# Square roots and residual sums as three-operand instructions on VectorE, and a new order for the scan layer's groups

## The chip, the cores and the metric

One core of a Trainium2 chip runs the whole kernel. The metric is the device time of one launch in microseconds, and less is better. The kernel before was timed ten times: the median is 15846.93 us, the runs lie between 15842.52 and 15853.14 us.

The core has five engines with queues of their own, each working strictly in its order: TensorE for matmuls (PE in the profile, its weight loads PEld), VectorE (DVE), ScalarE (ACT), GpSimd (POOL) and SyncE (SP, which here only issues DMAs). An instruction that waits holds up everything behind it on its engine.

## The reference

The input x is float32 of shape (8, 64, 128, 128). Four layers follow, each of the form x = x + layer(group norm of x):

```python
x = x + _L0_conv_ref(_gn(x), ...)   # offsets from 1x15 and 15x1 convolutions, deformable 3x3, batch norm, relu
x = x + _L1_conv_ref(_gn(x), L1_conv_weight)   # 3x3 convolution
x = x + _L2_conv_ref(_gn(x), ...)   # state-space scan over rows and over columns, both ways, then a 128 -> 64 fusion
x = x + _L3_conv_ref(_gn(x), ...)   # down by 4, nearest neighbours in a window, 3x3, attention, up by 4
```

The change is about the third layer. For each of two directions d it does

```python
fx = _layer_norm(x, ln1_g[i], ln1_b[i])        # over the 64 channels of a pixel
h = _s5_scan(fx, ...)                          # x[l] = lam_bar * x[l-1] + B u[l], forwards and backwards
x = jax.nn.gelu(h) + fx                        # the residual sum
fx2 = _layer_norm(x, ln2_g[i], ln2_b[i])       # the root: 1 / sqrt(var + 1e-5)
return fx2 @ ff_enc[i].T @ ff_dec[i].T + fx2
```

## The kernel before

Two images make a pair (2 x 64 channels on 128 partitions), so there are four pairs. Layer 0 runs first for all pairs: 9216 indirect gathers by POOL, each weighted and summed by VectorE. Then, pair by pair: `conv3x3` (layer 1; beside it, as `aside`, layer 3 of the pair before), `first_norm` with the first direction's backward scan (`back`) beside it, and `Turns`, which holds the rest of layer 2.

`Turns` works on two "ways" (the two directions), each cut into 16 groups of eight image rows or columns. One group is some fifty steps. They are put into one list with a due time each, the list is sorted by due time, and the instructions are emitted in that order (`run`, under `manual_schedule`, so nothing reorders them). A due time is the group's number times a length plus an entry of a table: `BESIDE` and the first number of `LENGTH` for the first way's 16 groups, beside which the second way's backward scan runs (`behind`, steps with a b at the end of the name); `ALONE` and the second number for the second way's 16 groups, beside which, in all pairs but the last, the next pair's input is loaded, passed through relu and added (`load`, `relu`, `join`, `sums`). The tables only set the order; a factor on a whole table with its length changes nothing.

A group's steps that matter below, by their names in the tables:

- `pv` (PE) applies the input matrix; `pt` (ACT) is `pv` with its halves swapped; `u` and `v` (VectorE, L1301, outputs `uu`, `uv`) multiply them by cosine and sine tables; `uv` (POOL, L1501) adds them; `scan` (VectorE, L1322) runs two first-order recurrences. `ub`, `vb`, `uvb` (L1555) and `scanb` are the same for the backward scan.
- `xm`, `xmb` (POOL, L1362) and `xt`, `xtb` (VectorE, L1367) rotate the states of the two scans back, `xs`, `xsb` (POOL, L1513 and L1512) subtract; `pya`, `pyb`, `pyc` (PE) apply the output matrices, for two halves h = 0 and 1.
- `gelu0`, `gelu1` (ACT), and `sum0`, `sum1` (L1522), the residual sums: both on VectorE in `ALONE`; in `BESIDE` `sum0` on VectorE and `sum1` on POOL.
- `pc` (PE) mixes, `sq` (ACT) squares and copies, `var` (VectorE, L1411) sums the squares. `root` (VectorE) is one call of `rsqrt` for both halves, 16 numbers on each partition: in the kernel before twelve instructions (L112, L114, L116 and three rounds of L120, L121, L122), each using the result of the one before it. `ms0` and `ms1` (POOL, L1416) scale by it, `tp` (PE) transposes, `add0` and `add1` (VectorE, L1428) add to the image.
- `stats` (L1436) and `sums` (L597) are bn_stats of finished rows on VectorE; `join` (POOL, L593) adds 128x1024 elements.

`rsqrt` is also called 32 times in `first_norm` with 32 numbers on a partition, read from PSUM (`by_pixel`), and about twenty times elsewhere with one number.

Of the kernel before, what the change touches and what calls it, by code (L numbers as in the profile page):

```python
# [9 lines left out]
F32 = mybir.dt.float32  # L10
I32 = mybir.dt.int32
AF = mybir.ActivationFunctionType
ALU = mybir.AluOpType
# [3 lines left out]
P = 128  # L17
# [25 lines left out]
class Net:  # L43
# [32 lines left out]

    def setup_constants(self):
        nc, const = self.nc, self.const
        with self.tc.tile_pool(name="setup", bufs=1) as sp:
            pid = self.iota(sp, "pid", [(0, 1)], mult=1)  # L80
            col = self.iota(sp, "col", [(1, P)])
            self.ident = const.tile([P, P], F32, name="ident")
            nc.vector.tensor_scalar(self.ident, col, pid, None, ALU.is_equal)

            pair_p = self.part_bits(sp, "pair_p", ALU.logical_shift_right, 1)
            pair_c = self.iota(sp, "pair_c", [(1, C), (0, 2)])
            self.pairmean = const.tile([P, P], F32, name="pairmean")
            nc.vector.tensor_scalar(self.pairmean, pair_c.rearrange("p a b -> p (a b)"), pair_p, 0.5, ALU.is_equal, ALU.mult)

            half_p = self.part_bits(sp, "half_p", ALU.bitwise_and, C - 1)  # L90
            half_c = self.iota(sp, "half_c", [(0, 2), (1, C)])
            self.halfmean = const.tile([P, P], F32, name="halfmean")
            nc.vector.tensor_scalar(self.halfmean, half_c.rearrange("p a b -> p (a b)"), half_p, 0.5, ALU.is_equal, ALU.mult)

            img_p = self.part_bits(sp, "img_p", ALU.logical_shift_right, 6)
            img_c = self.iota(sp, "img_c", [(1, 2), (0, C)])
            mean = sp.tile([P, P], F32, name="mean")
            nc.vector.tensor_scalar(mean, img_c.rearrange("p a b -> p (a b)"), img_p, 1.0 / C, ALU.is_equal, ALU.mult)
            self.center = const.tile([P, P], F32, name="center")
            nc.vector.tensor_sub(self.center, self.ident, mean)  # L100
            self.imgmean = const.tile([P, 2, 16], F32, name="imgmean")
            nc.vector.tensor_copy(self.imgmean, mean.rearrange("p (a b) -> p a b", b=C)[:, :, 0:16])
# [3 lines left out]
    def rsqrt(self, pool, v, n, eps, tag):  # L106

        nc = self.nc
        ve = pool.tile([P, n], F32, tag=tag + "_ve", name=tag + "_ve")

        to = ve if len(v.shape) == 2 else ve.rearrange("p (a b c) -> p a b c", b=v.shape[2], c=v.shape[3])
        nc.vector.tensor_scalar_add(to, v, eps)  # L112
        sh = pool.tile([P, n], I32, tag=tag + "_sh", name=tag + "_sh")
        nc.vector.tensor_single_scalar(sh, ve.bitcast(I32), 1, op=ALU.logical_shift_right)  # L114
        yi = pool.tile([P, n], I32, tag=tag + "_y", name=tag + "_y")
        nc.vector.tensor_scalar(yi, sh, -1.0, float(0x5F3759DF), ALU.mult, ALU.add)  # L116
        y = yi.bitcast(F32)
        t = pool.tile([P, n], F32, tag=tag + "_t", name=tag + "_t")
        for _ in range(3):
            nc.vector.tensor_mul(t, y, y)  # L120
            nc.vector.scalar_tensor_tensor(t, t, -0.5, ve, ALU.mult, ALU.mult)  # L121
            nc.vector.scalar_tensor_tensor(y, t, 1.5, y, ALU.add, ALU.mult)  # L122
        return y

# [1109 lines left out]
class Scan:  # L1234
# [146 lines left out]
    def hidden(self, g, h, py):  # L1381
        hs = self.wp.tile([P, 2, NB], F32, tag=f"h{h}", name=self.name(f"h{h}", 0, g), bufs=1)
        self.nc.scalar.activation(hs, py, AF.Gelu_apprx_tanh)
        return hs

    def mixed(self, g, h, hs, tag):

        nc = self.nc
        pc = [self.net.ps.tile([P, 4, 2, C], F32, tag=tag, name=self.name(f"pc{e}", h, g)) for e in range(2)]
        for m in range(2):  # L1390
            for i in range(2):
                for e in range(2):
                    rows = slice(e * C, (e + 1) * C)
                    both = self.mix[rows].rearrange("p (k e c) -> p k e c", k=2, e=2)[:, :, e]
                    nc.tensor.matmul(pc[e][:, 2 * m + i], lhsT=hs[rows, i, m * P : (m + 1) * P], rhs=both, start=True, stop=True)  # L1395
        return pc
# [52 lines left out]
class Turns:  # L1449


    BESIDE = dict(
        fx0=-42.405, fx1=-41.515, send=-40.807, zb=-28.652, pv=-26.364, pt=-21.441, u=-23.400, v=-17.007, uv=-14.705, pn=-20.678, z0=-18.245,
        scan=-13.543, zbt=-19.316, zt=-11.695, xmb=-10.926, xm=-11.234, xtb=-12.091, xt=-6.973, xsb=-6.185, xs=-3.151, pya=1.153, pyb=1.983,
        pyc=4.135, gelu0=4.021, sum0=5.398, pc0=8.273, sq0=10.755, var0=11.167, ms0=31.030, tp0=31.405, add0=40.135, gelu1=8.596, sum1=10.354,
        pc1=11.923, sq1=13.839, var1=20.715, ms1=39.583, tp1=44.833, add1=47.931, root=27.330, fxb0=-33.141, fxb1=-33.784, sendb=-31.014, pvb=-23.283,
        ptb=-19.852, ub=-14.630, vb=-14.109, uvb=-13.836, pnb=-9.910, z0b=-8.486, scanb=-5.226, save=-1.631,
    )
    ALONE = dict(
        fx0=-40.919, fx1=-37.171, send=-26.823, zb=-13.844, pv=-23.784, pt=-19.725, u=-18.742, v=-17.490, uv=-15.840, pn=-19.028, z0=-15.748,  # L1460
        scan=-12.765, zbt=-11.653, zt=-8.893, xmb=-7.844, xm=-11.490, xtb=-10.053, xt=-8.474, xsb=-7.169, xs=-4.677, pya=-2.975, pyb=0.799,
        pyc=11.316, gelu0=0.529, sum0=4.375, pc0=12.259, sq0=16.063, var0=19.019, ms0=34.253, tp0=41.960, add0=45.498, gelu1=16.070, sum1=21.691,
        pc1=22.877, sq1=27.017, var1=30.598, ms1=34.057, tp1=40.614, add1=44.609, root=31.015, store=94.689, stats=96.794, load=29.367, relu=46.454,
        join=51.618, sums=92.183,
    )
    LENGTH = 18.003, 17.817

    def __init__(self, net, ways, follow):
        self.net, self.ways, self.follow, self.plan = net, ways, follow, []
# [2 lines left out]
    def at(self, G, what, fn, late=0.0):  # L1472

        long, short = self.LENGTH
        t = (self.BESIDE, self.ALONE)[G >= NG][what]
        self.plan.append((min(G, NG) * long + max(0, G - NG) * short + t + late, len(self.plan), fn))

    def group(self, w, g):

        s, nc, G = self.ways[w], self.net.nc, NG * w + g  # L1480
        c, last, alone = {}, self.made.get((w, g - 1)), G >= NG
        self.made[w, g] = c

        def put(what, fn, key=None):
            def do():
                r = fn()
                if key:
                    c[key] = r

            self.at(G, what, do)  # L1490
# [24 lines left out]
        xs = lambda: [(1, c["x1"][0]), (0, c["x0"][0])]  # L1515
# [1 line left out]
        put("pyb", lambda: s.products(g, 1, None, None, xs(), True), "py1")  # L1517
        put("pyc", lambda: s.products(g, 1, c["py1"], c["in"], [], False))
        for h in range(2):
            adds = nc.gpsimd if h and not alone else nc.vector  # L1520
            put(f"gelu{h}", lambda h=h: s.hidden(g, h, c[f"py{h}"]), f"hs{h}")
            put(f"sum{h}", lambda h=h, adds=adds: adds.tensor_add(c[f"hs{h}"], c[f"hs{h}"], c["in"][:, :, h, :]))  # L1522
            put(f"pc{h}", lambda h=h: s.mixed(g, h, c[f"hs{h}"], "y" if h and not alone else "x"), f"pc{h}")
            put(f"sq{h}", lambda h=h: s.emptied(g, h, c[f"pc{h}"]), f"sq{h}")
            put(f"var{h}", lambda h=h: s.variance(g, h, c[f"sq{h}"][0], c.get("var")), "var")
            put(f"ms{h}", lambda h=h: s.scaled(h, c[f"sq{h}"][1], c["y"]))
            put(f"tp{h}", lambda h=h: s.flipped(g, h, c[f"sq{h}"][1], ("small", "bs")[h]), f"tp{h}")
            put(f"add{h}", lambda h=h: s.added(g, h, c[f"tp{h}"]))
# [100 lines left out]
```

## Time and profile before

| what | us |
|---|---|
| median of ten runs | 15846.93 |
| the profiled execution | 15841.47 |
| its span | 15839.7 |
| layer 0's gathers, first to last issue | 139.5 to 11665.8 |
| `Turns`, second pair: first gelu to last bn_stats | 13112.1 to 13640.8 |
| one group there in `BESIDE`, gelu0 to gelu0, settled | 16.8 |
| one group there in `ALONE`, settled | 15.5 |

```text
PE 10342.7 (65%) x32760; PEld 3743.6 (24%) x32760; DVE 11800.7 (75%) x27321; ACT 3260.7 (21%) x5530; POOL 10285.4 (65%) x10572
```

The line gives, for each engine, the time it was busy, its share of the span and its instructions. Shares over the whole span mix stages that have different limits; in `Turns` the profile has to be read for itself. A timeline row gives the start, the duration, the engine, the source line, the operation, output and inputs, their shapes, a count, and in brackets how long the engine had been idle and what ended that. VectorE instructions that don't depend on each other overlap slightly: the next one's start comes some 0.08 us before the recorded end of the one before, so a step is counted from start to start.

### The profile page before, as it was taken

The numbers are of one execution on the slowest core, as the hardware profiler recorded it, in microseconds if no ns is written. First come the engines' busy times: TensorE is split into PE (matmuls) and PEld (weight loads), VectorE is DVE, ScalarE is ACT, GpSimd is POOL, SyncE is SP. The second block draws the span as 40 slices with busy tenths as digits, with TensorE's granted clock in tenths as the row PEclk, the third lists the DMA queues.
The fourth block names the chain that finished last, engine by engine and source line by source line (L and its number), as shares of the span: only waits on it lengthen the run. The fifth ranks groups of instructions, "written<-read, shape, count | busy, mean of one in ns | idle before, by whom it ended". The sixth has DMA issues, their size and how long they took to land. (4 is left out here: it accounts for less than half of the span.)

```text
span 15839.7 us, 121589 instructions
## 1 busy us (share of the span) xinstructions
PE 10342.7 (65%) x32760; PEld 3743.6 (24%) x32760; DVE 11800.7 (75%) x27321; ACT 3260.7 (21%) x5530; POOL 10285.4 (65%) x10572
## 2 busy tenths in 40 slices
PE   7864577447755553776656556664258788888886
PEld 2211122112211111221111111111123434434343
DVE  6777777777777777777777777777756858679587
ACT  1100111011100000110000000000016537366373
POOL 5777777777777777777777777777744506236052
PEclk9986798669877775987878778886569999999998
DMA  5444444345443333544333333333333433434434
GB/s 173 125 121 134 132 148 154 114 126 157 152 118 114 115 116 116 153 137 119 113 115 119 115 115 116 115 115 108 108 119 84 132 106 101 123 113 124 113 90 114
DMA packets 901297, 1933.56 MB, mean 122 GB/s; under 512 B 200060, under 2 KB 436996, under 8 KB 877572
## 3 DMA queue, kind: packets, MB, share of 16 engines
q0 software_dynamic: 442368, 1208.55, 26.3%
q1 hardware_dynamic: 383200, 679.50, 14.2%
q10 hardware_dynamic: 75044, 37.72, 1.3%
q8 instruction: 265, 4.34, 0.1%
q14 instruction: 420, 3.44, 0.1%
HBM read 1540.74 MB, written 208.10 MB: 110 GB/s over the span
## 5 line engine op out<-in xcount | busy, mean ns | idle before, releaser
L380 POOL DMA_INDIRECT g<-table,idx x9216 | 8718.3, 946 | 2822.9 <-issue 2631.7
L391 DVE TENSOR_TENSOR g<-g,corner_weights 128x256 f32<-128x256 f32 x9216 | 3765.4, 415 | 2713.4 <-DMA g<-table,idx 2674.2
L392 DVE TENSOR_REDUCE sm<-g 128x64 f32<-128x256 f32 x9216 | 5012.6, 579 | 9.0
L292 PE MATMUL po<-xe,wt 128*54 128x512 f32 (+3 forms) x8384 | 4307.1, 629 | 14.3 <-ACT ob L302 13.7
L398 PE MATMUL sp<-ident,sm 128*128 128x128 f32 x4096 | 1537.5, 380 | 4147.8 <-DVE sm L392 4133.5
L403 ACT COPY s<-sp 128x512 f32<-128x512 f32 x1024 | 598.6, 585 | 8703.1 <-PE sp L398 8702.8
L398 PEld LDWEIGHTS sp<-ident,sm 128*128 128x128 f32 x4096 | 630.6, 156 | 6710.2 <-DVE sm L392 5004.5
L292 PEld LDWEIGHTS po<-xe,wt 128*54 128x54 f32 x8384 | 904.3, 132 | 1354.1 <-issue 1070.8
L409 PE MATMUL yp<-s,wd 128*64 128x512 f32 (+1 forms) x2560 | 902.8, 714 | 25.6 <-ACT s L403 24.8
L924 POOL COPY l_yb<-ln_y 128x512 f32<-128x512 f32 x128 | 76.4, 637 | 1241.7 <-DVE ln_y L122 1241.7
L641 PE MATMUL c<-room,l_w 128*64 128x508 f32 (+1 forms) x3072 | 738.7, 606 | 44.1 <-DMA room<-nx 28.3
L1272 ACT ACTIVATE fx<-room,ln_b,ln_g 128x512 f32<-128x512 f32 x512 | 646.0, 1300 | 94.0 <-DMA in<-fx 76.2
L1288 PE MATMUL pv<-in,tabs 128*128 128x512 f32 x1024 | 546.4, 660 | 88.4 <-DMA in<-fx 43.1
L1378 PE MATMUL py<-in,outs 128*128 128x512 f32 x1024 | 519.5, 632 | 1.8 <-ACT ms L1405 1.7
L1378 PE MATMUL py<-x,outs 128*128 128x512 f32 x1024 | 477.7, 601 | 0.0
L1416 POOL TENSOR_TENSOR ms<-ms,ln_y 128x512 f32<-128x512 f32 x256 | 268.3, 1058 | 271.1 <-DVE ln_y L122 268.8
L1322 DVE TENSOR_TENSOR_SCAN z<-tabs,z,uu 128x256 f32<-128x256 f32 x512 | 405.9, 830 | 42.8 <-POOL uu L1338 40.2
L1395 PE MATMUL pc<-mix,h 64*128 64x128 f32 x4096 | 318.3, 297 | 135.7 <-DVE h L1522 95.8
L641 PEld LDWEIGHTS c<-room,l_w 128*64 128x64 f32 x3072 | 287.5, 139 | 384.8 <-issue 313.8
L402 PE MATMUL s<-ident,sm 128*64 128x128 f32 x512 | 176.6, 345 | 306.3 <-DVE sm L392 293.1
L643 DVE TENSOR_TENSOR room<-room,c 128x512 f32<-128x512 f32 x128 | 87.3, 684 | 372.0 <-PE c L641 368.8
L409 PEld LDWEIGHTS yp<-s,wd 128*64 128x64 f32 (+1 forms) x2560 | 261.6, 159 | 433.0 <-issue 316.3
(422 smaller groups left out, 10328.0 us busy)
## 6 DMA issues: line engine op xcount, KB each, us to landing
g<-table,idx POOLq DMA_INDIRECT x9216, 2.7
in<-fx SPq DMA_DIRECT2D x1024, 128.0 KB
xe<-in_x_dram SPq DMA_DIRECT2D x56, 1408.0 KB
table<-q SPq DMA_DIRECT2D x256, 256.0 KB
y<-ys SPq DMA_DIRECT2D x128, 256.0 KB
room<-in_x_dram SPq DMA_DIRECT2D x64, 512.0 KB
room<-nx SPq DMA_DIRECT2D x256, 128.0 KB
back<-z SPq DMA_DIRECT2D x128, 256.0 KB
```

The costliest lines, as they stand in the source:

```text
L292: nc.tensor.matmul(po[:, r0:r1, c0:c1], lhsT=wt[:, t, :], rhs=xe[:, row + r0 : row + r1, c0 + dx : c1 + dx], start=n == 0, stop=n == len(u ...
L380: nc.gpsimd.indirect_dma_start(out=tq[:, k, :], out_offset=None, in_=flat[i], in_offset=bass.IndirectOffsetOnAxis(ap=idx[:, at : at + 1], ...
L391: nc.vector.tensor_mul(t[:, ks], t[:, ks], w)
L392: nc.vector.tensor_reduce(sm[:, ks], t[:, ks].rearrange("p k q c -> p k c q"), axis=mybir.AxisListType.X, op=ALU.add)
L398: nc.tensor.transpose(sp[:, j, :], sm[:, j * P : (j + 1) * P], self.ident)
L403: nc.scalar.copy(st[i][:, :, m * P : (m + 1) * P], sp)
L409: nc.tensor.matmul(yp[half[i], :], lhsT=wd[rows, j, :], rhs=src[rows, :], start=j == 0, stop=j == 4)
L641: nc.tensor.matmul(o, lhsT=lt, rhs=mv, start=k < 2, stop=k >= len(calls) - 2)
L1272: self.nc.scalar.activation(fx[:, e].rearrange("p h (o m) -> p h o m", m=self.INNER), src, AF.Identity, bias=self.w["ln1_b"], scale=self.w ...
L1288: self.nc.tensor.matmul(pv, lhsT=self.tabs[:, at : at + P], rhs=fx[:, :, h, :], start=h == 0, stop=h == 1)
L1322: self.nc.vector.tensor_tensor_scan(z[:, i, 1 : NB + 1], decay, u[:, i, :], z[:, i, 0:1], ALU.mult, ALU.add)
L1378: self.nc.tensor.matmul(py, lhsT=lt, rhs=mv, start=first and n == 0, stop=n == len(calls) - 1 and (fx is not None))
```

## The change

`rsqrt` gets by without VectorE's one-input and two-operand forms: each of its instructions is now a scalar_tensor_tensor, (in0 op scalar) op in1. The logical shift disappears, since -0.5 times the bits, read as an integer, plus a constant does both steps. So eleven instructions stand where twelve stood. The constant comes from a one-column tile `magic`. Where the input has four dimensions (`first_norm`, in PSUM) the first instruction stays as it was. The residual sums on VectorE take the same form. Both tables and the lengths are replaced.

```diff
+        self.magic = const.tile([P, 1], F32, name="magic")
+        nc.vector.memset(self.magic, float(0x5F3759DF))
...
-        to = ve if len(v.shape) == 2 else ve.rearrange("p (a b c) -> p a b c", b=v.shape[2], c=v.shape[3])
-        nc.vector.tensor_scalar_add(to, v, eps)
-        sh = pool.tile([P, n], I32, tag=tag + "_sh", name=tag + "_sh")
-        nc.vector.tensor_single_scalar(sh, ve.bitcast(I32), 1, op=ALU.logical_shift_right)
+        if len(v.shape) == 2:
+            nc.vector.scalar_tensor_tensor(ve, v, eps, v, ALU.add, ALU.max)
+        else:
+            nc.vector.tensor_scalar_add(ve.rearrange("p (a b c) -> p a b c", b=v.shape[2], c=v.shape[3]), v, eps)
         yi = pool.tile([P, n], I32, tag=tag + "_y", name=tag + "_y")
-        nc.vector.tensor_scalar(yi, sh, -1.0, float(0x5F3759DF), ALU.mult, ALU.add)
+        nc.vector.scalar_tensor_tensor(yi, ve.bitcast(I32), -0.5, self.magic.to_broadcast([P, n]), ALU.mult, ALU.add)
...
         for _ in range(3):
-            nc.vector.tensor_mul(t, y, y)
-            nc.vector.scalar_tensor_tensor(t, t, -0.5, ve, ALU.mult, ALU.mult)
+            nc.vector.scalar_tensor_tensor(t, y, -0.5, y, ALU.mult, ALU.mult)
+            nc.vector.scalar_tensor_tensor(t, t, 1.0, ve, ALU.mult, ALU.mult)
             nc.vector.scalar_tensor_tensor(y, t, 1.5, y, ALU.add, ALU.mult)
...
+    def summed(self, hs, x, aside):
+        if aside:
+            self.nc.gpsimd.tensor_add(hs, hs, x)
+        else:
+            self.nc.vector.scalar_tensor_tensor(hs, hs, 1.0, x, ALU.mult, ALU.add)
...
     BESIDE = dict(
-        fx0=-42.405, fx1=-41.515, send=-40.807, zb=-28.652, pv=-26.364, pt=-21.441, u=-23.400, v=-17.007, uv=-14.705, pn=-20.678, z0=-18.245,
+        fx0=-45.652, fx1=-47.679, send=-42.514, zb=-23.890, pv=-31.014, pt=-22.829, u=-25.279, v=-19.908, uv=-18.338, pn=-21.924, z0=-20.467,
...
-    LENGTH = 18.003, 17.817
+    LENGTH = 21.546, 24.354
...
-            put(f"sum{h}", lambda h=h, adds=adds: adds.tensor_add(c[f"hs{h}"], c[f"hs{h}"], c["in"][:, :, h, :]))
+            put(f"sum{h}", lambda h=h: s.summed(c[f"hs{h}"], c["in"][:, :, h, :], h and not alone))
```

What the tables become on the two engines that matter, one settled period (steps of several groups):

```text
BESIDE  VectorE before  root xt var0 add1 u scanb v var1 ub vb add0 scan sum0 xtb
        VectorE after   root xt u var0 add1 scanb v ub vb var1 scan add0 sum0 xtb
        POOL before     ms0 xs uv ms1 uvb xm xmb sum1 xsb
        POOL after      ms0 xs ms1 uv uvb xm xmb sum1 xsb
ALONE   VectorE before  root u v var0 sums sum1 sum0 scan stats xtb add1 xt add0 var1
        VectorE after   root u v sum1 add0 stats scan var0 sums xtb xt sum0 add1 var1
        POOL before     ms1 ms0 uv xm xmb xsb xs join
        POOL after      uv ms1 xm xmb xsb ms0 xs join
```

On PE and ACT the order in `BESIDE` changes in a few places (pv before tp1; z0 and z0b later or earlier by some steps); in `ALONE` PE runs tp0 pn pya pyb pc1 tp1 pyc pv pc0, where it ran pyb tp1 pc1 tp0 pyc pv pc0 pya pn.

More of the change, by code (lines that the diff above doesn't have):

```diff
@@ L1452 @@
     BESIDE = dict(
-        fx0=-42.405, fx1=-41.515, send=-40.807, zb=-28.652, pv=-26.364, pt=-21.441, u=-23.400, v=-17.007, uv=-14.705, pn=-20.678, z0=-18.245,
-        scan=-13.543, zbt=-19.316, zt=-11.695, xmb=-10.926, xm=-11.234, xtb=-12.091, xt=-6.973, xsb=-6.185, xs=-3.151, pya=1.153, pyb=1.983,
-        pyc=4.135, gelu0=4.021, sum0=5.398, pc0=8.273, sq0=10.755, var0=11.167, ms0=31.030, tp0=31.405, add0=40.135, gelu1=8.596, sum1=10.354,
-        pc1=11.923, sq1=13.839, var1=20.715, ms1=39.583, tp1=44.833, add1=47.931, root=27.330, fxb0=-33.141, fxb1=-33.784, sendb=-31.014, pvb=-23.283,
@@ L1457 @@
-        ptb=-19.852, ub=-14.630, vb=-14.109, uvb=-13.836, pnb=-9.910, z0b=-8.486, scanb=-5.226, save=-1.631,
+        fx0=-45.652, fx1=-47.679, send=-42.514, zb=-23.890, pv=-31.014, pt=-22.829, u=-25.279, v=-19.908, uv=-18.338, pn=-21.924, z0=-20.467,
+        scan=-17.477, zbt=-21.716, zt=-10.595, xmb=-13.956, xm=-16.483, xtb=-12.386, xt=-6.541, xsb=-8.637, xs=-4.189, pya=3.246, pyb=4.850,
+        pyc=5.035, gelu0=4.068, sum0=8.411, pc0=10.360, sq0=12.619, var0=18.195, ms0=35.736, tp0=42.572, add0=49.502, gelu1=6.165, sum1=11.369,
@@ L1458 @@
+        pc1=13.025, sq1=19.116, var1=24.577, ms1=45.304, tp1=55.515, add1=62.138, root=32.998, fxb0=-39.102, fxb1=-39.291, sendb=-33.449, pvb=-27.769,
+        ptb=-22.659, ub=-19.512, vb=-19.321, uvb=-17.665, pnb=-14.526, z0b=-8.897, scanb=-1.320, save=0.599,
     )
     ALONE = dict(
-        fx0=-40.919, fx1=-37.171, send=-26.823, zb=-13.844, pv=-23.784, pt=-19.725, u=-18.742, v=-17.490, uv=-15.840, pn=-19.028, z0=-15.748,
-        scan=-12.765, zbt=-11.653, zt=-8.893, xmb=-7.844, xm=-11.490, xtb=-10.053, xt=-8.474, xsb=-7.169, xs=-4.677, pya=-2.975, pyb=0.799,
@@ L1462 @@
-        pyc=11.316, gelu0=0.529, sum0=4.375, pc0=12.259, sq0=16.063, var0=19.019, ms0=34.253, tp0=41.960, add0=45.498, gelu1=16.070, sum1=21.691,
-        pc1=22.877, sq1=27.017, var1=30.598, ms1=34.057, tp1=40.614, add1=44.609, root=31.015, store=94.689, stats=96.794, load=29.367, relu=46.454,
-        join=51.618, sums=92.183,
+        fx0=-51.767, fx1=-41.682, send=-37.725, zb=-16.016, pv=-29.340, pt=-19.974, u=-20.804, v=-19.806, uv=-19.540, pn=-22.227, z0=-19.605,
+        scan=-17.335, zbt=-15.589, zt=-14.503, xmb=-14.133, xm=-14.265, xtb=-11.591, xt=-10.011, xsb=-7.864, xs=-5.653, pya=4.831, pyb=7.800,
@@ L1465 @@
+        pyc=13.782, gelu0=9.353, sum0=14.661, pc0=20.405, sq0=30.528, var0=33.864, ms0=65.653, tp0=73.515, add0=78.834, gelu1=24.228, sum1=30.085,
+        pc1=33.967, sq1=41.979, var1=46.643, ms1=56.716, tp1=61.026, add1=65.309, root=48.888, store=88.626, stats=79.551, load=24.511, relu=38.822,
+        join=43.314, sums=107.607,
     )
-    LENGTH = 18.003, 17.817
+    LENGTH = 21.546, 24.354
     def __init__(self, net, ways, follow):
@@ L1519, in group @@
         for h in range(2):
-            adds = nc.gpsimd if h and not alone else nc.vector
             put(f"gelu{h}", lambda h=h: s.hidden(g, h, c[f"py{h}"]), f"hs{h}")
-            put(f"sum{h}", lambda h=h, adds=adds: adds.tensor_add(c[f"hs{h}"], c[f"hs{h}"], c["in"][:, :, h, :]))
+            put(f"sum{h}", lambda h=h: s.summed(c[f"hs{h}"], c["in"][:, :, h, :], h and not alone))
             put(f"pc{h}", lambda h=h: s.mixed(g, h, c[f"hs{h}"], "y" if h and not alone else "x"), f"pc{h}")
```

## The prediction

> **What bounds the kernel now.** The busy shares by stage come first. Here are two settled stretches of the second pair, six groups in BESIDE and ten in ALONE; columns: stretch, its length, busy time of PE, PEld, DVE, ACT and POOL with their instructions, granted clock, DMA share, GB/s.
>
> ```profile
> 13193.90:13294.60 100.70, 91.10 (x409) 47.20 (x408) 98.44 (x163) 77.95 (x145) 65.98 (x54) 0.97 0.38 95
> 13433.40:13588.70 155.30, 132.30 (x621) 70.95 (x620) 151.18 (x277) 101.35 (x200) 106.98 (x82) 0.95 0.50 153
> ```
>
> VectorE is busy 98% and 97%, and no VectorE row there has idle time of note before it: VectorE sets the pace. Next is PE; its work, from the starts of its rows with its waits taken out, is 14.7 us of BESIDE's 16.8 us and 12.5 us of ALONE's 15.5 us. The second view is the timeline of both engines around a root in BESIDE (start, duration).
>
> ```profile
> 13211.32 0.66 DVE L1522 TENSOR_TENSOR h<-h,in 128x512 f32<-128x512 f32 x1
> 13211.90 0.68 DVE L1367 TENSOR_TENSOR xt<-pt,tabs 128x512 f32<-128x512 f32 x1
> 13212.50 0.63 DVE L112 TENSOR_SCALAR ln_ve<-var 128x16 f32<-128x16 f32 x1
> 13213.17 1.20 DVE L114 TENSOR_SCALAR ln_sh<-ln_ve 128x16 int32<-128x16 int32 x1
> 13214.40 1.19 DVE L116 TENSOR_SCALAR ln_y<-ln_sh 128x16 int32<-128x16 int32 x1
> 13215.62 1.19 DVE L120 TENSOR_TENSOR ln_t<-ln_y 128x16 f32<-128x16 f32 x1
> 13216.85 0.18 DVE L121 SCALAR_TENSOR_TENSOR ln_t<-ln_t,ln_ve 128x16 f32<-128x16 f32 x1
> ...
> 13211.56 1.54 POOL L1362 TENSOR_TENSOR x<-z,tabs 128x512 f32<-128x512 f32 x1 [1.36 <-PE pn L1307]
> 13213.07 1.27 POOL L1362 TENSOR_TENSOR x<-zb,tabs 128x512 f32<-128x512 f32 x1
> 13214.30 1.26 POOL L1522 TENSOR_TENSOR h<-h,in 128x512 f32<-128x512 f32 x1
> 13215.52 1.27 POOL L1512 TENSOR_TENSOR x<-x,xt 128x512 f32<-128x512 f32 x1
> 13218.57 1.05 POOL L1416 TENSOR_TENSOR ms<-ms,ln_y 128x512 f32<-128x512 f32 x1 [1.79 <-DVE ln_y L122]
> ```
>
> Sixteen numbers take 0.17 us, but four of the root's instructions take 0.63 to 1.20, and each ends 0.02 or 0.03 us after a POOL instruction ends. POOL has four instructions queued ahead of ms0; when they are through, POOL waits for the root, and the other eight run freely. In ALONE the same is seen with POOL's `join`:
>
> ```profile
> 13506.86 0.28 DVE L112 TENSOR_SCALAR ln_ve<-var 128x16 f32<-128x16 f32 x1
> 13507.18 2.28 DVE L114 TENSOR_SCALAR ln_sh<-ln_ve 128x16 int32<-128x16 int32 x1
> 13509.49 0.17 DVE L116 TENSOR_SCALAR ln_y<-ln_sh 128x16 int32<-128x16 int32 x1
> ...
> 13505.84 1.27 POOL L1513 TENSOR_TENSOR x<-x,xt 128x512 f32<-128x512 f32 x1
> 13507.08 2.35 POOL L593 TENSOR_TENSOR room<-room,yr 128x1024 f32<-128x1024 f32 x1
> ```
>
> In these stretches L121 and L122, already three-operand, take 0.17 or 0.18 us every time. That looks like immunity, but they run when POOL has nothing left to do. Where one does start inside a POOL instruction, it waits too; in the first norm:
>
> ```profile
> 11991.03 1.30 POOL L1338 TENSOR_TENSOR uu<-uu,uv 128x512 f32<-128x512 f32 x1 [4.24 <-DVE ln_y L116]
> ...
> 11991.23 1.14 DVE L121 SCALAR_TENSOR_TENSOR ln_t<-ln_t,ln_ve 128x32 f32<-128x32 f32 x1
> ```
>
> It ends 0.04 us after POOL. This meeting occurs eight times in the scan layers (twice in each pair) and costs 1.14 to 1.15 us each time.
>
> **The change part by part.** *One instruction fewer in a root*: start to start, a free one is 0.21 us (13216.85 to 13217.06), on VectorE, which bounds: -0.21 us in each of 128 groups. In the first norm it is on the chain root, POOL copy, PE: 32 x 0.21 = -6.7 us if nothing covers it, 0 if the scan beside it does; I take the first. About twenty other roots are single: 20 x 0.2 = 4 us at most, and those in layer 0 lie beside gathers; I take 0.
>
> *The form*: with POOL idle a three-operand instruction takes what the others take (0.17 us). With POOL busy, eight meetings of eight show the wait, for 128x32 with two different inputs. That one tile given twice, or 128x512, waits too is shown for two-operand forms only: L120 (one tile twice) and L1522. So I take the wait as unchanged. Bounds: all gone, or all there.
>
> The Trainium skill bears on this, "SBUF — State Buffer", section "Who interferes with whom": an instruction of VectorE with two inputs in SBUF contends with a GpSimd instruction that reads SBUF, and this speaks against any gain from the form, for the cases that no row shows too. The section says as well that the loser "fully blocks" until the first finishes; a 128x512 instruction would then need its whole 0.7 us afterwards, while the rows show 0.54. By the rule the sum below, which has two long meetings more in each BESIDE group than the kernel before, would be 2 x 0.16 x 64 = 20 us longer; the rows decide.
>
> *The new order*, walked through with three prices from rows. A short instruction that meets POOL ends 0.04 us after it. A long one (scan, sum) ends 0.54 us after it: the scan at 13209.46 ends at 10.75, uvb at 10.21. POOL waits for a long one that is running (xm 1.54 instead of 1.27). Inputs from PSUM don't meet POOL: L1301 takes 0.68 us either way.
>
> BESIDE. Starts to starts, the old period is 12.75 of work and 4.05 of waits (root 3.5, scan 0.56) = 16.8. In the new order, let add0 start at 0, the scans having ended at 0.08. POOL's xm runs 0.24 to 1.51; sum0 comes at 1.13 and, waiting for xm, ends at 2.05; xmb, held by it, ends at 3.20. xtb runs 1.97 to 2.57. The root starts at 2.57 and meets xmb (to 3.24), sum1 (4.47) and xsb (5.70), three instead of four, then has eight free steps: xt starts at 7.3. ms0 ends at 8.6, xs at 9.8, and ms1, now next, at 10.84. xt, u, var0, add1 take until 10.23, so scanb meets ms1: 11.38 instead of 10.96. v, ub, vb, var1 end at 14.4; uv and uvb run 12.8 to 15.3, so scan meets uvb: 15.84. The next add0 starts at 16.4. **-0.4 us a group, x 64 = -26 us.** PE must be ready for pc0 at 2.2 + 16.4: from add1's end (10.3) pn and the three py take 7.5, so 17.8: 0.8 us to spare.
>
> ALONE with the next pair's input. Old: 12.95 of work + 2.55 of waits (L114 2.1, L112 0.1, sum1 0.35) = 15.5. New, from scan's end: var0, both sums and xtb until 2.4, xt until 3.0; xm, xmb, xsb run 0.16 to 3.9, so sum0 ends at 4.44; ms0, held by it, ends at 5.4, xs at 6.6, join at 8.95. add1 and var1 end at 6.07. The root meets xs (6.63) and join (8.96), nine free steps take it to 10.8; u, v until 12.0, sum1 12.6, add0 13.6, stats 14.8, scan 16.2. **+0.7 us a group, x 48 = +34 us.** Behind this wait on VectorE stand u and v, so pt, zbt and gelu0 on ACT, and tp1 on PE (after ms1): PE is then idle 3.7 us of 16.2, so it doesn't bind. The last pair has no join and no sums: the same walk gives 13.9 against 13.3 to 13.7 in the rows; +0.4 x 16 = +6 us.
>
> *Head, turn and tail of Turns*: fx, send, fxb, sendb come in the same order and start the same chain. At the turn the load of `outs` waits on SP for pyc of group 15, and the load of zb and a send stand behind it; VectorE is then idle 6.5 us (before 13368.42). In the new tables zb 16 is again due just after that load, so this stays: 0, +-3 us a pair. Fewer stats and sums are left for the tail; they filled waits for PE (0.5 and 1.2 us at 13611 and 13623): 0 to +3 us a pair.
>
> Sum: -6.7 - 26 + 34 + 6 = +7 us. Against its own execution: 15841.5 + 7 = 15849; that execution lies 5.5 us below the median, so **15855 us**. With +-0.4 us a group in BESIDE (26 us) and +-0.5 in ALONE (32 us), its own range is 15815 to 15895.
>
> **The rivals.** *Three operands are immune.* For it: L122 never waits in 480 executions. Against: the eight meetings. Then BESIDE would be bound by PE at 14.7 to 15 (-1.9 x 64 = -122) and ALONE by VectorE at 12.95 - 0.2 or PE, about 13 (-2.5 x 48, and -0.5 x 16): -128. With the first norm's -7 that is -257: 15590 us.
>
> *Slower: the fourth meeting stays.* The gain in BESIDE rests on xm running beside add0. If xm starts more than 1.1 us late (the row puts its release at pn on PE), xmb, sum1 and xsb all move back and the root meets four instructions, while ms1 and uvb still meet the scans: 16.4 + 1.05 = 17.45, +0.65 x 64 = +42, with ALONE's +40 and the first norm's -7: 15920 us. For it: PE's 0.8 us to spare is thin. Against: xm needs only scan and a free tile.
>
> *Faster: join comes late.* If relu on ACT is done only after the root has begun, join isn't there to meet it, and runs beside u and v, which read PSUM. The root then saves 2.1 us and sum1 loses some 0.5 to it: -1.6 x 48 = -77, so +7 - 77 = -70: 15777 us. For it: in ALONE of the second pair join waited for relu 10 us in all. Against: in the walk relu is done at 2.5 and join can't start before 6.6; it takes 4 us of delay before this decides.
>
> *The change doesn't do what it says*: the tables move only the order, and where all engines wait for VectorE the order gives the same sum. Then only the instructions count: -27 - 7, 15813 us.
>
> **How the numbers follow.** Forecast 0.54, immune 0.06, fourth meeting 0.23, late join 0.10, instructions only 0.07. Less than 0.2% (32 us) can't be told from no change here. The forecast splits into 0.05 faster, 0.35 within, 0.14 slower; immunity and the late join are faster, the fourth meeting is slower, and the last case lies at the edge, 0.04 and 0.03. Faster 0.25, same 0.38, slower 0.37. The range for 8 in 10 runs from 15775 (late join) to 15930 (fourth meeting); it leaves out immunity and what lies beyond those two.
>
> **What would show it.** In the new profile: L121-like rows of the root at 0.6 to 2.3 us, three a root in BESIDE and two in ALONE, each ending with POOL; sum0 at 0.9 us or more; gelu0 to gelu0 16.4 in BESIDE and 16.2 in ALONE; VectorE still 97% busy. Wrong: roots of eleven rows of 0.17 us beside busy POOL (immune), or idle time on VectorE in settled groups, ended by PE or ACT (an order that starves it).

## The result and the profile after

The kernel after takes 15933.85 us (median of 8 runs, 15928.52 to 15936.54) against 15847.59 us for the kernel before (28 runs): a ratio of 1.0054, 95% interval 1.0045 to 1.0063, so it is 86 us slower. Its profiled execution spans 15925.0 us, the one before 15839.7 us.

From the starts of the gelu rows, group 0 of a pair to group 0 of the next, the 85 us are made up like this (four pairs, 15 intervals each in BESIDE and in ALONE; "the end" is here and below the end of VectorE's last instruction, 5 us before the end of the span):

| stretch, summed over the pairs | before | after | difference |
|---|---|---|---|
| BESIDE, first to last gelu0 | 985.6 | 975.2 | -10 |
| turn, last gelu0 of BESIDE to first of ALONE | 83.7 | 88.0 | +4 |
| ALONE, first to last gelu0 | 869.9 | 996.4 | **+126** |
| from there to the next pair's first gelu0 (tail, group norm, convolution, first norm) | 1549.4 | 1524.6 | -25 |
| last gelu0 to the end | 240.8 | 229.9 | -11 |

All of the loss lies in ALONE. Settled, a group takes 16.6 us in BESIDE (16.8 before, 16.4 predicted); in ALONE it takes 17.8 us with the next pair's input (15.1 before, 16.2 predicted) and 15.4 us in the last pair (13.0 before, 13.9 predicted).

The busy times of two settled stretches of the second pair after, six groups in BESIDE and ten in ALONE, in the columns that the prediction used (length, then PE, PEld, DVE, ACT, POOL):

```profile
13201.70:13301.20 99.50, 88.93 (x409) 46.15 (x408) 95.48 (x157) 77.80 (x145) 67.52 (x54) 1.00 0.38 96
13451.60:13629.30 177.70, 142.32 (x623) 75.11 (x620) 160.09 (x269) 103.09 (x201) 114.70 (x83) 0.90 0.43 134
```

VectorE was busy 97% of ALONE; now it is 90%. It is no longer only slow, it stands idle. The timeline of one ALONE group after shows where, and which parts of the walk came true (VectorE, then ACT, then POOL):

```profile
13562.53 1.69 DVE L1391 SCALAR_TENSOR_TENSOR h<-h,in 128x512 f32<-128x512 f32 x1
...
13565.86 0.52 DVE L113 SCALAR_TENSOR_TENSOR ln_ve<-var 128x16 f32<-128x16 f32 x1
13566.42 2.27 DVE L117 SCALAR_TENSOR_TENSOR ln_y<-ln_ve,magic 128x16 int32<-128x16 int32 x1
13568.72 0.17 DVE L121 SCALAR_TENSOR_TENSOR ln_t<-ln_y 128x16 f32<-128x16 f32 x1
...
13570.48 0.68 DVE L1302 TENSOR_TENSOR uu<-pv,tabs 128x512 f32<-128x512 f32 x1
13572.51 0.69 DVE L1302 TENSOR_TENSOR uv<-pt,tabs 128x512 f32<-128x512 f32 x1 [1.34 <-ACT z L1317]
...
13564.23 0.59 ACT L1384 ACTIVATE h<-py 128x512 f32<-128x512 f32 x1
13571.26 1.15 ACT L1261 COPY pt<-pv 64x512 f32<-64x512 f32 x2 [6.44 <-DVE uu L1302]
...
13562.40 1.27 POOL L1519 TENSOR_TENSOR x<-x,xt 128x512 f32<-128x512 f32 x1
...
13565.08 1.27 POOL L1520 TENSOR_TENSOR x<-x,xt 128x512 f32<-128x512 f32 x1
13566.31 2.35 POOL L594 TENSOR_TENSOR room<-room,yr 128x1024 f32<-128x1024 f32 x1
```

The three-operand sum0 beside `xsb` takes 1.69 us, L113 beside `xs` 0.52, L117 beside join 2.27, and the root's other nine rows 0.17 or 0.18: these are the walk's meetings, one for one. What the walk doesn't have is the 1.34 us ahead of v (`uv`). It is put down to a tiny `z` copy, but that row ran at 13572.33, behind `pt`; what v reads is `pt`. And `pt`, two copies on ACT that swap the halves of `pv`, starts 0.09 us after u (`uu`) has ended, after ACT has stood idle for 6.44 us, though `pv` was ready on PE at 13564.05. In all 56 ALONE groups whose u lies between the first and the last gelu0 of ALONE, over the four pairs, `pt` starts 0.09 us after u's end; in the kernel before it started 1.9 to 6.5 us ahead of u's end. One such place of the kernel before (VectorE, then ACT), with v right behind u:

```profile
13526.99 0.68 DVE L1301 TENSOR_TENSOR uu<-pv,tabs 128x512 f32<-128x512 f32 x1
13527.59 0.68 DVE L1301 TENSOR_TENSOR uv<-pt,tabs 128x512 f32<-128x512 f32 x1
...
13522.07 1.15 ACT L1260 COPY pt<-pv 64x512 f32<-64x512 f32 x2
```

The rows of these copies over ten ALONE groups add it up, first before, then after:

```profile
L1260 ACT COPY pt<-pv 64x512 f32<-64x512 f32 x20 | 11.2, 558 | 6.4 <-PE pv L1288 5.9
L1261 ACT COPY pt<-pv 64x512 f32<-64x512 f32 x20 | 11.2, 558 | 64.4 <-DVE uu L1302 64.1
```

After, ACT is idle for 64 us ahead of these copies, all put down to u. The waits recorded in the trace say the same: after, the first `pt` copy of a group waits for VectorE and ACT, and u for PE alone; before, the copy waits for PE and for an older VectorE instruction, since it runs ahead of u, and it is u that waits for ACT. Both only read `pv`. So the schedule puts these two readers of one PSUM tile in the order in which they are issued, though they run on different engines; e3 and e9 below turn that order round. In the diff, ALONE's u went from 0.98 behind `pt` (-18.742 against -19.725) to 0.83 ahead of it (-20.804 against -19.974).

### The profile page after: what moved, and what is told of

Same layout as the page of the kernel before. It is cut to its first block, busy times and chain, and to the rows that moved or that the text cites. A ratio compares the mean times of both kernels' runs of the same rounds, so it can differ in the third digit from the quotient of the medians.

```text
span 15925.0 us, 121497 instructions
## 1 busy us (share of the span) xinstructions
PE 10367.6 (65%) x32760; PEld 3735.5 (23%) x32760; DVE 11779.7 (74%) x27142; ACT 3255.3 (20%) x5530; POOL 10329.2 (65%) x10572
## 5 line engine op out<-in xcount | busy, mean ns | idle before, releaser
L1508 POOL TENSOR_TENSOR uu<-uu,uv 128x512 f32<-128x512 f32 x128 | 184.7, 1443 | 448.3 <-DVE uv L1302 432.7
L1261 ACT COPY pt<-pv 64x512 f32<-64x512 f32 x512 | 285.7, 558 | 455.5 <-DVE uu L1302 353.1
```

## The experiments

Twelve kernels were run, in three sets: e1 to e4, e5 to e8, e9 to e12. In the second and third set, on another chip than the first, the gathers of layer 0, which no kernel here changes, took about 3000 us longer for every kernel, the kernel before among them (18892 and 18996 us); the later stages did not (BESIDE 16.6 us in e6 as in e3). So besides the ratio to the kernel before in the same set, the table gives the interval from the first gelu0 to the end of the one profiled execution of each kernel, and gelu0 to gelu0 (the median of a pair, its first interval left out; pairs one to three for ALONE, then the last pair).

| kernel | ratio, 95% interval | first gelu0 to end | BESIDE | ALONE | last ALONE |
|---|---|---|---|---|---|
| before | 1 | 3729.6 | 16.8 | 15.0-15.1 | 13.0 |
| after | 1.0054, 1.0045-1.0063 | 3814.1 | 16.6 | 17.8 | 15.4 |
| e1 operations alone | 0.9977, 0.9968-0.9986 | 3694.7 | 16.6 | 14.9-15.4 | 12.6 |
| e2 order alone | 1.0078, 1.0064-1.0092 | 3850.0 | 16.8 | 18.0 | 15.6 |
| e3 `pt` ahead of u | 1.0008, 0.9999-1.0017 | 3742.1 | 16.6 | 16.4 | 13.9 |
| e4 old ALONE | 0.9979, 0.9970-0.9988 | 3687.3 | 16.6 | 14.9-15.1 | 13.1 |
| e5 ms0 early | 0.9998, 0.9931-1.0064 | 3710.3 | 16.2 | 16.4 | 13.9 |
| e6 join late | 0.9956, 0.9908-1.0003 | 3734.9 | 16.6 | 15.7-16.1 | 13.9 |
| e7 both, old order | 1.0007, 0.9949-1.0065 | 3742.2 | 16.5-17.5 | 15.2-15.4 | 12.5 |
| e8 root clear | 1.0082, 1.0022-1.0142 | 3845.0 | 18.9 | 15.2-15.4 | 12.6 |
| e9 u ahead, old order | 1.0031, 1.0017-1.0045 | 3766.1 | 16.6 | 16.6 | 14.5 |
| e10 join on VectorE | 0.9961, 0.9944-0.9978 | 3647.9 | 16.6 | 13.8-14.1 | 12.5 |
| e11 and two more | 0.9979, 0.9963-0.9995 | 3661.4 | 16.6 | 13.9-14.1 | 12.9 |
| e12 and three more | 0.9961, 0.9948-0.9974 | 3647.5 | 16.5 | 14.0-14.1 | 12.8 |

**The two halves of the change, one at a time.** e1 has the new operations with both old tables and LENGTH; e2 has the old operations with the new ones.

> The tables of due times and LENGTH are those of the kernel before; only the operations are the changed kernel's (root in eleven three-operand instructions, sums on VectorE in three-operand form). Theory (the form waits for POOL as the two-operand form does, and only the instruction saved counts): 0.21 us less in each of 128 groups and up to 7 us less in the first norms: BESIDE 16.6 and ALONE 14.9 us from gelu0 to gelu0 (16.8 and 15.05 before), 15813 to 15820 us against 15847. Rival 1 (three operands don't meet POOL): the root's waits of 3.5 us in BESIDE and 2.2 us in ALONE go, about 15590 us. Rival 2 (the form itself is what cost the 86 us): 15900 us or more.

> The operations of the kernel before (twelve instructions a root, two-operand sums) in the new order: the changed kernel's tables and LENGTH. Theory (all of the loss is the order's): the changed kernel's time and 0.2 us more in each of 128 groups, 15934 + 27 to 34 = 15960 to 15970 us; ALONE about 18.0 us from gelu0 to gelu0, with VectorE idle 1.3 us between u and v. Rival (the form of the operations loses it): near the kernel before, 15850 us.

e1 took 15809.75 us, e2 15971.21 us, against 15846.57 us for the kernel before in the same set. So the operations gain 37 us and the order loses 125. One instruction fewer in a root is worth what the prediction said where the order is the same: BESIDE goes from 16.8 to 16.6 us, and ALONE in the new order from 18.0 to 17.8 us (e2 to the kernel after). That e1's 37 us agree with the expected 27 to 34 is in part luck, though. By the stretches of the first table e1 gains 14 us in BESIDE, only 4 us in ALONE, where 60 x 0.21 would be 13, and 17 us in the two stretches behind ALONE, where up to 7 had been expected. The three-operand form doesn't escape POOL.

**The missed wait, taken out and put in.** e3 is the kernel after with one number changed; the order on VectorE, ACT and POOL is the same, except that u and one add change places once in each pair, early in ALONE, and the direction of the wait between two readers of `pv` turns.

```diff
-fx0=-51.767, fx1=-41.682, send=-37.725, zb=-16.016, pv=-29.340, pt=-19.974, u=-20.804, v=-19.806, ...
+fx0=-51.767, fx1=-41.682, send=-37.725, zb=-16.016, pv=-29.340, pt=-19.974, u=-19.900, v=-19.806, ...
```

> The changed kernel with one due time altered: in ALONE u is due just behind pt instead of just ahead of it, so that the order on every engine stays and only the wait changes: u waits for pt on ACT and no longer pt for u. Theory (pt stands idle on ACT for 6.4 us until u has run behind the root, and VectorE is then idle 1.34 us before v; this is the missed term): ALONE 17.8 - 1.34 = 16.4 us, 64 x 1.34 = 86 us less than the changed kernel, 15848 us. Rival (ALONE is set by the root's meetings with xs and join or by another engine, and the idle time only moves to another place): within 15 us of the changed kernel's 15934.

15860.38 us: 73 us less than the kernel after, of the 86 expected. ALONE takes 16.4 us and 13.9 us in the last pair. The same place in e3 (VectorE, then ACT):

```profile
13557.86 0.68 DVE L1302 TENSOR_TENSOR uu<-pv,tabs 128x512 f32<-128x512 f32 x1
13558.46 0.68 DVE L1302 TENSOR_TENSOR uv<-pt,tabs 128x512 f32<-128x512 f32 x1
...
13552.20 1.15 ACT L1261 COPY pt<-pv 64x512 f32<-64x512 f32 x2
```

`pt` now runs 5.7 us ahead of u, while VectorE is still at its root, and v follows u at once. e9 is the converse: e1, whose ALONE is the old one, with u's due time put ahead of `pt`'s; again the order of the scan layers on VectorE, ACT and POOL is unchanged.

```diff
-fx0=-40.919, fx1=-37.171, send=-26.823, zb=-13.844, pv=-23.784, pt=-19.725, u=-18.742, ...
+fx0=-40.919, fx1=-37.171, send=-26.823, zb=-13.844, pv=-23.784, pt=-19.725, u=-19.750, ...
```

> The converse of e3_pt_first: e1_ops_alone with one due time altered, in ALONE u just ahead of pt (-19.750 instead of -18.742). The order on every engine is that of e1_ops_alone; only pt now waits for u. Theory (pt, 1.15 us on ACT, starts 0.09 us behind u, and v behind it): VectorE idle 1.34 us in each ALONE group, 64 x 1.34 = 86 us more than e1_ops_alone, 15895 us. Rival (the old order has slack there, u stands early enough): within 15 us of e1_ops_alone's 15810.

From the first gelu0 to the end it takes 71 us more than e1, and 0.31% more than the kernel before, where 0.30% was expected. In its rows the same gap stands, this time put down to `pt` itself:

```profile
16689.42 0.68 DVE L1302 TENSOR_TENSOR uu<-pv,tabs 128x512 f32<-128x512 f32 x1
16691.45 0.69 DVE L1302 TENSOR_TENSOR uv<-pt,tabs 128x512 f32<-128x512 f32 x1 [1.34 <-ACT pt L1261]
...
16690.20 1.15 ACT L1261 COPY pt<-pv 64x512 f32<-64x512 f32 x2 [4.21 <-DVE uu L1302]
```

**Which table holds the loss.** e4 is the kernel after with ALONE's table and length of the kernel before.

> The changed kernel with ALONE and its LENGTH of the kernel before; operations and BESIDE stay changed. Theory (ALONE's order holds the loss of some 126 us, BESIDE's order and the first norms hold a gain of some 40): 15934 - 126 - 64 x 0.2 = 15795 us, ALONE 14.9 us, BESIDE 16.6 us. Rival (BESIDE's gain or the head's needs the new ALONE behind it, as work moved across the turn): 15820 to 15850 us.

15814.0 us: 120 us less than after, but 19 us more than the theory said, and no better than e1 (15809.75 us), which has the old BESIDE as well. So all of the loss is ALONE's, and BESIDE's new order by itself brings nothing.

**Moving the root's meetings.** Four kernels move due times so that the root meets fewer POOL instructions: e5 and e6 from e3, e7 and e8 from e1.

```diff
 e5, BESIDE:  -ms0=35.736  +ms0=33.000
 e6, ALONE:   -join=43.314 +join=56.758
 e7, BESIDE:  -ms0=31.030  +ms0=27.331   ALONE: -join=51.618 +join=52.120
 e8, e7 with  -root=27.330, ms0=27.331   +root=24.770, ms0=24.771
```

> e3_pt_first with one more due time: in BESIDE ms0 on POOL is due just behind the root (33.000), so that it stands ahead of sum1 and xsb in POOL's queue and POOL stops for the root after xmb. Theory (each meeting of a root's instruction with POOL costs VectorE, which bounds, about 1.03 us): the root meets xmb alone, 2 x 1.03 = 2.06 us of waits go, until PE binds at 14.7 to 15: BESIDE 14.7 to 15.0 us instead of 16.6, 15860 - 64 x 1.6 to 1.9 = 15740 to 15760 us. Rival (sum1 and xsb, some 3.3 us later on POOL, starve pc1 and the py on PE, and the waits come back as idle time of VectorE): BESIDE 16.4 us or more, 15850 us or more.

> e3_pt_first with join in ALONE due behind the root's ms1 (56.758 instead of 43.314), so that the root meets xs alone. Theory (the meeting with join is worth 2.1 us of VectorE's 16.4): ALONE with the next pair's input 14.3 to 14.8 us (up to 0.5 comes back where join now meets a sum or a scan), 15860 - 48 x 1.6 to 2.1 = 15760 to 15785 us. Rival (join meets as much at its new place, or another engine binds): ALONE 16 us or more, 15840 us or more.

> e1_ops_alone (the old tables, the new operations) with ms0 ahead of sum1 and xsb in BESIDE (27.331) and join behind ms0 in ALONE (52.120). Theory of the meetings: in BESIDE two of the root's four meetings go, 16.6 - 2.06 = 14.5, PE then binds at 14.7 to 15; in ALONE the root meets nothing, 15.1 - 2.1 = 13.0, with up to 0.5 back: 13.0 to 13.6. 15810 - 64 x 1.6 to 1.9 - 48 x 1.5 to 2.1 = 15590 to 15635 us. Rival (PE or POOL takes over at once): 15780 us or more.

> e7_both_late with root and ms0 in BESIDE due ahead of xm (24.770 and 24.771), so that the root runs beside a POOL that waits for it, and meets nothing but what is left of uvb. Theory (only VectorE's waits count until PE binds): as e7_both_late within 20 us, since PE binds both. Rival (xm, xmb, xsb and xs start some 3 us later, so that the py on PE are starved): 50 us or more above e7_both_late.

All four fell short of the theory of the meetings. e5 gained 0.4 us in BESIDE instead of 1.6 to 1.9; e6 some 0.2 us (237 us instead of 240 for 15 intervals) instead of 1.6 to 2.1; e7 next to nothing in ALONE (861 us instead of 866 in e1, over the four pairs) and a loss in BESIDE; e8 lost 2.3 us a group in BESIDE, where VectorE stands idle for 3.9 us a group ahead of v, until `pt` is done. In e6, e7 and e8 the times are those of the rival named beforehand. Here is what became of join's meeting in e6 (VectorE, then POOL):

```profile
16465.02 3.38 DVE L1323 TENSOR_TENSOR_SCAN z<-tabs,z,uu 128x256 f32<-128x256 f32 x2
...
16464.86 2.35 POOL L594 TENSOR_TENSOR room<-room,spare 128x1024 f32<-128x1024 f32 x1
```

The root no longer meets join; the scans do, and take 3.38 us instead of the 1.38 they take in e3. In e7 the two sums met join (3.80 us for both at 16561.19), and the root still met `xs`.

e5 did not do all that its expectation says. Counted from the next group, sum1 is due at 11.369 + 21.546 = 32.915, just ahead of ms0's 33.000, so ms0 passed `xsb` alone and POOL ran xm, xmb, sum1, ms0, `xsb`. The root then met two instructions instead of three, not one: from start to start it took 1.02 us less a group. The scans met `xs` and ms1 and took 1.0 us more. The 0.4 us that e5 did gain are another wait, which went as a side effect: ub's wait for ptb, of which more below. So here a meeting that was moved away came back, at its full price.

That suggests another count. Take as *occupied* the time in which POOL runs, or VectorE runs something whose inputs all lie in SBUF (root, scans, sums, join; not the statistics, which don't wait for POOL), and as *free* the rest. From the rows of the second pair, us a group, over eight settled groups of BESIDE and nine of ALONE:

| | before | after | e1 | e3 | e5 | e6 | e8 | e10 | e11 |
|---|---|---|---|---|---|---|---|---|---|
| BESIDE occupied | 15.2 | 15.05 | 15.0 | 15.05 | 14.95 | 15.05 | 15.3 | 15.0 | 13.9 |
| BESIDE free | 1.6 | 1.5 | 1.6 | 1.5 | 1.2 | 1.5 | 3.65 | 1.6 | 2.7 |
| ALONE occupied | 14.9 | 14.6 | 14.7 | 14.6 | 14.6 | 14.6 | 14.6 | 13.55 | 13.55 |
| ALONE free | 0.7 | 3.2 | 0.65 | 1.8 | 1.8 | 1.7 | 0.75 | 0.6 | 0.6 |

With the same division of the work (all but e10 and e11) the occupied time stays within 0.4 us, whatever the order; e2, e4, e7 and e9, counted in the same way, lie within these bounds too. Only the free time moves. The loss of the kernel after in ALONE is 2.5 us of free time, of which e3 takes back 1.4 us.

**Work moved instead of meetings.** If the sum of the two engines counts, an instruction that VectorE does in half of POOL's time should pay.

```diff
 e10: join
-                nc.gpsimd.tensor_add(af[:, s], af[:, s], rooms[n])
+                nc.vector.tensor_add(af[:, s], af[:, s], rooms[n])
 e11: also sum1 and xsb in BESIDE; e12: also xs
-        put("xsb", lambda: nc.gpsimd.tensor_sub(c["x1"][1], c["x1"][1], c["xtb"]))
+        put("xsb", lambda: (nc.gpsimd if alone else nc.vector).tensor_sub(c["x1"][1], c["x1"][1], c["xtb"]))
```

> e1_ops_alone with join (128x1024, 2.35 us on POOL) on VectorE. Theory (work on POOL and VectorE's work on inputs from SBUF shut each other out, so that their sum, not the order, sets ALONE: 14.7 us of 15.4 in e1_ops_alone have one of the two running): join takes about 1.2 us of VectorE instead of 2.35 of POOL, so 15.4 - 1.15 = 14.2 us in ALONE with the next pair's input, 48 x 1.15 = 55 us less, 15755 us. Rival (VectorE's own work is the bound): 1.2 us more a group less the root's wait of 2.1, or, if the root's wait only moves, 48 x 1.2 = 58 us more, 15868 us.

> e10_join_dve with sum1 and xsb of BESIDE on VectorE as well (0.66 us each there, 1.27 on POOL). Theory (one of the two engines at a time): 15.05 - 2 x 0.61 = 13.8 us occupied in BESIDE; VectorE's own work rises to 13.9 and PE's is 14.7, so 15.0 to 15.4 us instead of 16.6, 64 x 1.2 to 1.6 = 77 to 102 us less than e10_join_dve, 15655 to 15680 us. Rival (VectorE's queue, 98% busy, only grows longer): 64 x 1.2 = 77 us more.

> e11_two_dve with BESIDE's xs on VectorE too. Theory: 13.2 us occupied in BESIDE, VectorE's own work 14.5, PE 14.7: 14.8 to 15.3 us, so 0 to 20 us less than e11_two_dve. Rival (VectorE is full, or py waits for xs in VectorE's queue): 30 us or more above e11_two_dve.

e10 did in ALONE what the count says: join takes 1.22 us on VectorE instead of 2.35 on POOL, and the occupied time falls by 1.15 us and the settled group to about 14.1 us. From the first gelu0 to the end it takes 47 us less than e1 (55 expected), all of it in ALONE; the ratios of the whole program, 0.9961 and 0.9977, come from different sets and don't tell the two apart. e11 failed in BESIDE: the occupied time fell by 1.1 us as expected, but free time took its place and the group stayed at 16.6 us. One settled stretch of six groups of e11, and from its first group `xsb` on VectorE and `xs` on POOL:

```profile
16331.66:16431.50 99.84, 86.71 (x409) 46.51 (x408) 97.78 (x169) 77.92 (x145) 53.81 (x42) 1.00 0.38 96
...
16338.95 1.58 DVE L1519 TENSOR_TENSOR x<-x,xt 128x512 f32<-128x512 f32 x1
...
16338.71 1.28 POOL L1520 TENSOR_TENSOR x<-x,xt 128x512 f32<-128x512 f32 x1
```

POOL is busy 12.5 us less than in six groups of e10 (66.27 us), and VectorE still 98%. From start to start, the root meets two POOL instructions instead of four, 2.04 us less a group; but sum1 and `xsb` are 2 x 0.60 us of new work, and `xsb` meets `xs` and so takes 0.9 us longer than a free one. That fills it up again: VectorE's queue binds, with own work of 13.9 us (the estimate of e11's expectation) and some 2.7 us of waits in it. e12 gained 0.1 us a group in BESIDE (16.5, where 14.8 to 15.3 were expected): its occupied time fell to 13.4 us, and its free time rose to 3.1. In the interval from the first gelu0 to the end e10 and e12 are the shortest; both, by their ratios, are faster than the kernel before, and the kernel after is slower than it.

## Why the prediction was wrong

The predicted 15855 us lies below the measured 15934 us, and its range ends 4 us short of it.

**The step that failed** is ALONE's walk, "nine free steps take it to 10.8; u, v until 12.0", with the sentence behind it: "Behind this wait on VectorE stand u and v, so pt, zbt and gelu0 on ACT, and tp1 on PE ...: PE is then idle 3.7 us of 16.2, so it doesn't bind." It asked whether PE would be starved, not whether v would. It even names `pt` among what stands behind u, yet it runs u and v back to back, 1.2 us for both, as in the rows of before, as if `pt` were ready when VectorE came to v. The tables turn the order of u and `pt`, so that `pt` now starts behind u: root, u, `pt`, v are one chain, 1.34 us of it with VectorE idle. Of the signs that the prediction gave for itself being wrong, this is the second, "idle time on VectorE in settled groups, ended by PE or ACT"; but no rival had a price for it. With that one wait taken out (e3) the walk's numbers come out: 16.4 us for 16.2, 13.9 us for 13.9, and 15860 us for 15855. The wait cost 73 us (after to e3) and 71 us (e1 to e9). What e3 keeps of ALONE's loss, 59 of the 126 us, is the longer group that the walk did foresee, at 40.

The Trainium skill has the rule that was missed, "PSUM — Partial Sum Buffer", section "PSUM bank collisions raise a hardware error": two engines must not touch one bank and partition quadrant at once, two reads included, so that such instructions are put in an order. The rows here agree with the order, with `pt` 0.09 us behind u; what would happen without it no run here shows.

The other steps:

- *One instruction fewer*, -0.21 us a group: right, 0.2 us in both stages in the new order; in the old order ALONE gained less than 0.1 us a group (e1). In the first norm it didn't come: from the first `l_yb` copy to the last the second pair takes 116.7 us before, 119.2 after, 120.8 in e1 and 116.4 in e2. The new operations cost 2 to 4 us a pair there instead of gaining 1.7; which of the norm's waits grew was not followed up.
- *The form waits for POOL*: right, and now also shown where it was only assumed, for one tile given twice and for 128x512. (The 1.14 to 1.15 us of the prediction's eight meetings are the whole row; a free one takes 0.19, so a meeting costs 0.95.) In the first norm after, L121 with one tile given twice beside POOL:

```profile
13036.72 1.15 DVE L121 SCALAR_TENSOR_TENSOR ln_t<-ln_y 128x32 f32<-128x32 f32 x1
...
13036.51 1.31 POOL L1339 TENSOR_TENSOR uu<-uu,uv 128x512 f32<-128x512 f32 x1 [6.97 <-DVE ln_ve L115]
```

The sum in ALONE (13562.53) ends 0.55 us after `xsb`, as the two-operand sums before did with 0.54 to 0.55, and not a whole 0.7 us later.

- *BESIDE*, 16.4: its meetings came as walked, three for the root, one each for sum0 and two scans. The 0.2 us missing are of the same kind as ALONE's: ub waits for ptb, issued ahead of it, on ACT. (VectorE of the kernel after, one BESIDE group:)

```profile
13213.68 0.66 DVE L1302 TENSOR_TENSOR uv<-pt,tabs 128x512 f32<-128x512 f32 x1
13214.67 0.69 DVE L1302 TENSOR_TENSOR uu<-pv,tabs 128x512 f32<-128x512 f32 x1 [0.33 <-ACT pt L1261]
...
13221.01 0.64 DVE L113 SCALAR_TENSOR_TENSOR ln_ve<-var 128x16 f32<-128x16 f32 x1
13221.69 1.20 DVE L117 SCALAR_TENSOR_TENSOR ln_y<-ln_ve,magic 128x16 int32<-128x16 int32 x1
13222.92 1.20 DVE L121 SCALAR_TENSOR_TENSOR ln_t<-ln_y 128x16 f32<-128x16 f32 x1
```

  This wait was not tried by itself, but in e5, where ub follows v at once, it is gone, and the root's gain and the scans' loss cancel: the group takes 16.2 us, 0.4 less. So the wait costs more than the 0.2 us that were missing, and the rest of the walk was some 0.2 us too long. The whole gain there is the instruction's; the order gives none (e1 and after are both at 16.6).
- *Tail*, 0 to +3 us a pair, and nothing in the sum: wrong in sign. The stretch behind ALONE's last gelu0 got 7.7 to 9.0 us shorter between pairs and 10.9 us at the end; the new order alone (e2) makes it 4.4 to 7.3 and 5.8 us shorter, the operations alone (e1) 3.3 to 4.0 and 6.4. Part of this is only where gelu0 stands in a group; with it, e3's ALONE and tails are together 22 us longer than before, where the walk had 40. The old group of 15.5 us, against which the walk set its 16.2, was too long as well: the median of a pair is 15.0 to 15.1. So e3's agreement with 15855 has errors of some 20 us in it that cancel.
- *The rivals*: immunity is refuted by e1; the fourth meeting and the late join did not happen (three meetings in BESIDE; join runs at 13566.31, 0.11 us ahead of L117). "Only the instructions count", 15813 us, is what e1 and e4 measure (15810 and 15814 us), but not the kernel after, since its order does cost.

## What to carry to other kernels

When an order is changed, list for every tile its readers on all engines, not only its writer: here two engines that read one PSUM tile were put in the order of issue, and the second one inherited whatever the first was queued behind. Where VectorE and POOL shut each other out, a meeting that was moved away here came back elsewhere; count the time in which one of the two is at it, which the order hardly changed, and shorten that by moving work to the engine that does it in half the time, as long as that engine's own queue has room (ALONE in e10, not BESIDE in e11).

## What the runs showed of the hardware

Two things stand out. The statistics instruction on VectorE (two rows in 1.28 us at 16463.82 in e6, with ms1 running on POOL from 16463.86 to 16464.90) isn't held up, while a root's instruction on 16 numbers is; so it is not VectorE's use of SBUF as such that waits. And the occupied time of VectorE and POOL together stayed at 14.6 to 14.9 us in ALONE and 14.95 to 15.3 us in BESIDE over every order tried with the same division of the work: the form of the instruction and its place made no difference to it, only which engine did the work.
